# The head of a Mamba block and a mixture of experts: B of the first chunk by TensorE, a split silu

## The chip, the cores and the metric

The kernel runs on one core of one Trainium2 chip. The metric is device time in microseconds (us), the median of several executions. A profile is one more execution, recorded by the hardware profiler.

The engines are TensorE (PE; PEld is its weight load), VectorE (DVE), ScalarE (ACT), GpSimd (POOL) and SyncE (SP), which here only issues transfers (DMAs). Each engine works through its own instructions in the order of the program and waits on semaphores for the others.

## The reference

All arrays are float32; x is 4 x 512 x 256.

```
def mamba(x):                                   # d_inner 512, 16 states, convolution of 4, dt rank 16
    xc, gate = split(x @ in_proj_w.T)
    xt = silu(causal_depthwise_conv(xc) + conv_b)
    ts, B, C = split(xt @ x_proj_w.T, [16, 32])
    dt = softplus(ts @ dt_proj_w.T + dt_proj_b)
    state = state * exp(dt * A) + dt * B * xt   # scanned over the 512 tokens
    y = (state @ C + xt * D) * silu(gate)
    return y @ out_proj_w.T

def moe(x):                                     # 16 experts, the best 4 per token, and a shared one
    ...

x = x + layernorm(mamba(layernorm(x)))
x = x + layernorm(moe(layernorm(x)))
```

## The kernel before

The tokens are cut into 8 tiles of 256 (U), two to a sequence. The 512 channels are four chunks of 128. The scan (L778) works on 128 partitions that hold 32 channels by 4 states; a slot is two such groups of channels by 256 tokens, so that a tile of tokens has 32 slots. For each slot ScalarE computes exp(dt * A) into PSUM (exps, L493), GpSimd multiplies dt * x by B (dbx, L505, one instruction for two slots), VectorE scans (L778) and multiplies by C (hc, L786), and TensorE sums over the states (L800). For this dt and u = dt * x must be spread from 128 channels to 32 channels by 4 states (the tile rep), and B and C from rows to all partitions (bt and ct). Both go through DRAM: stored (L385, L448), then read back with a broadcast (load_rep, L477; load_bc, L470).

Beside the scan of one tile of tokens runs the front of the next ones (norm, in_proj L391, convolution L406, silu L423, x_proj L434, dt_proj L457, softplus L463) and the experts of those before (L1042, L1077 on TensorE; L1049 to L1064 on the others). A planner in the kernel (class Plan) lays down the order of all that from given durations and ranks. It takes the head's state from fixed figures (BUSY) and knows nothing of what the head contains.

The head is written out by hand (function first) and handles tile 0 until its first two slots. In order: layer norm, transposes, taps, in_proj, convolution. Then for both pairs of chunks a sigmoid on ScalarE (two tanh, L414, and one Copy over both chunks that makes 0.5 t + 0.5, L418), then silu on VectorE (L423). A one-element Softplus (L542) loads that table. x_proj (L434) follows, with TensorE's warm-ups (L313, matmuls of the identity) between its parts: four after the second chunk, two after the fourth. Its output becomes ssm on ScalarE (L442): rows of tokens' dt rank, B and C, for the first 128 tokens on the lower 64 partitions and for the others on the upper 64. The store of B and C (L448) and dt_proj (L457) read it. Four more warm-ups into bank f follow, then softplus (L463).

load_bc(0) reads B and C back from DRAM as bt and ct. GpSimd makes u for the first chunk (L553). For this chunk alone dt and u are not spread through DRAM but by TensorE: eight matmuls with a matrix of zeros and ones (rsel, L561) into banks f, h3, y and po, which VectorE copies into rep (L564): f and h3 are dt and u of the first two groups of channels, y and po those of the other two. Then GpSimd multiplies u by B in two halves (inputs_of(0, 2), L505), each for one slot: the first reads what came out of h3, the second what came out of po. Behind them in its queue stand u of the second chunk (L568), the next product (L505), u of the last two chunks (L573), and then the planner's order.

Eight banks of PSUM are in use: three for exps, and f, y, h1, h3 and po, one each; a new tile in a bank waits for the readers of the one before. SBUF tiles come from rings (RINGS): a name has so many buffers, taken in turn.

Of the kernel before, what the change touches and what calls it, by code (L numbers as in the profile page):

```python
# [9 lines left out]
F32 = mybir.dt.float32  # L10
AF = mybir.ActivationFunctionType
ALU = mybir.AluOpType
AX = mybir.AxisListType

P = 128
# [3 lines left out]
R = 16  # L19
# [6 lines left out]
U = 256  # L26
# [4 lines left out]
SS = 4  # L31
CS = P // SS
SG = NS // SS
CG = P // CS
# [14 lines left out]
RINGS = dict(  # L49
    x=3, xr=2, xn=1, xn_t=3, xp=3, sig=2, xt=4, gate=2, ssm=2, dt=1, u=2, mv=6, rstd=6,  # L50
    tail=4, bt=2, ct=2, xg=2, rep=3, delta=3, h=3, dbx=3, hc=11, yg=2, o=1, xn2=1, xn_t2=2, lg=2,
    cw=2, cw_t=1, w13=3, w2=4, cwb=4, th=2, g=3, q=2, res=1, f=1, y=1, h1=1, h3=1, po=1,
)
# [50 lines left out]
    fin=(0.3, 1, 2.2, 1, 0.6, 2.2, 1.5, 0.1),  # L104
)

GROUPS = dict(
    fA=(1, "x stats rstd norm transpose evict"),
    fB=(1, "pad0 in tail conv sigmoid silu xg0"),
# [21 lines left out]
)  # L131
GROUP_OF = {kind: (g, per) for g, (per, kinds) in GROUPS.items() for kind in kinds.split()}


def shift_of(name):
    kind = name[0] + str(name[2]) if name[0] == "xg" else name[0]
    g, per = GROUP_OF[kind]
    n = name[1] // per
    return SHIFTS[g][n] if g in SHIFTS else 0.0, PATIENCE[g][n] if g in PATIENCE else 0.1


class Plan:
# [21 lines left out]

    def add(self, name, eng, dur, rank, fn, deps=(), alloc=(), uses=(), kb=0, done=None):
        shift, patience = shift_of(name)
        rank += shift
        t = dict(
            name=name, eng=eng, dur=dur, rank=rank, fn=fn, deps=[self.names[d] for d in deps],
            alloc=alloc, kb=kb, done=done, at=len(self.tasks), patience=patience,  # L170
        )
        assert name not in self.names, name
        self.names[name] = t
        self.tasks.append(t)
        for key in [key for _, key in alloc] + list(uses):
            self.users.setdefault(key, []).append(t)
        return t
# [70 lines left out]
def mamba_then_moe(ctx: ExitStack, tc: tile.TileContext, a: dict, out: bass.AP):  # L248
    nc = tc.nc
    V, S, G, T = nc.vector, nc.scalar, nc.gpsimd, nc.tensor  # L250
# [5 lines left out]
    work = ctx.enter_context(tc.tile_pool(name="work", bufs=1))  # L256
    dram = ctx.enter_context(tc.tile_pool(name="dram", bufs=N, space=bass.MemoryType.DRAM))
    ps_e = ctx.enter_context(tc.tile_pool(name="ps_e", bufs=RINGS["h"], space=PSUM))
    ps = ctx.enter_context(tc.tile_pool(name="ps", bufs=1, space=PSUM))
# [6 lines left out]
    def load_x(n, what=xs, nm="x"):  # L266
        what[n] = work.tile([P, NU, D], F32, name=nm, bufs=RINGS[nm])
        nc.sync.dma_start(out=what[n], in_=x_in[:, n])
# [21 lines left out]

    rsel = work.tile([P, CG, P], F32, name="w2", bufs=4)
    nc.sync.dma_start(out=rsel, in_=a["rsel"])
    for n in range(1, 3):
        load_x(n)
    w_out = const.tile([P, CI, D], F32, name="w_out")
# [14 lines left out]
    def warm(n, bank):  # L310
        t = ps.tile([P, P], F32, name=bank)
        for _ in range(n):
            T.matmul(t, ident, ident, start=True, stop=True)  # L313
# [6 lines left out]
    hb = const.tile([P, CI], F32, name="hb")  # L320
# [6 lines left out]
    def make_taps():  # L327
        for c in range(CI):
            for k in range(KC):
                V.tensor_scalar_mul(taps[:, c, k, :], ident2, chan[:, c, k : k + 1])  # L330
# [7 lines left out]
    def stats_of(t):  # L338

        st = stat.tile([P, 2, 3], F32, name="st", bufs=RINGS["mv"])  # L340
        V.bn_stats(st.rearrange("p i k -> p (i k)"), t.rearrange("p i d -> p d i"))
        return st
# [21 lines left out]
    live, q = {}, {}  # L364
# [7 lines left out]
    def ring(pool, shape, nm):  # L372
        return pool.tile(shape, F32, name=nm, bufs=RINGS[nm])
# [13 lines left out]
    def in_proj(n, m, bank):  # L387
        t = q["in", n, m] = ps.tile([P, 2, U], F32, name=bank)
        for j in range(2):
            for k in range(CD):  # L390
                T.matmul(  # L391
                    t[:, j, :], w_in[:, k, ts(2 * m + j, P)], q["xn_t", n][:, k, :],
                    start=k == 0, stop=k == CD - 1,
                )
# [16 lines left out]
    def sigmoid(n, m):  # L411
        t = q["sig", n, m]
        for j in range(2):
            S.activation(  # L414
                t[:, j, :], q["conv", n, m][j], AF.Tanh,
                scale=0.5, bias=hb[:, 2 * m + j : 2 * m + j + 1],
            )
        S.activation(t, t, AF.Copy, scale=0.5, bias=0.5)  # L418

    def silu(n, m):  # L420
        t = q["xt", n, m]
        for j in range(2):
            V.scalar_tensor_tensor(  # L423
                t[:, j, :], q["conv", n, m][j], conv_b[2 * m + j], q["sig", n, m][:, j, :],
                ALU.add, ALU.mult,
            )
# [14 lines left out]
    def ssm(n):  # L441
        S.activation(q["ssm", n], q["x", n], AF.Identity, bias=one_row)  # L442
# [40 lines left out]
    def place(k):  # L483

        return k // SLOTS, k // CSL % CI, k // CP % SG, k % CP
# [9 lines left out]
        for j in range(1, NJ):  # L495
            S.copy(h[:, j, 0:1], zero)  # L496

    def inputs_of(k, parts=1):

        n, c, g, _ = place(k)  # L500
        t = dbxs[k // CP] = ring(work, [P, CG, U], "dbx")
        bt = live[n]["bt"][:, g, :].unsqueeze(1).to_broadcast([P, CG, U])
        for i in range(parts):
            m = ts(i, CG // parts)
            G.tensor_tensor(t[:, m], reps[n * CI + c][:, m, 1, :], bt[:, m], ALU.mult)  # L505
        if n % UB:
            G.tensor_tensor(t[:, :, 0], t[:, :, 0], deltas[n * CI + c][:, g, :], ALU.add)

    def first():
        st = stats_of(xs[0])  # L510
        rstd = stat.tile([P, NU], F32, name="rstd")
        G.tensor_scalar(rstd, st[:, :, 2], 1.0 / D, EPS, ALU.mult, ALU.add)
        G.tensor_tensor(rstd, rstd, mhalf, ALU.pow)
        xn = ring(work, [P, NU, D], "xn")
        for i in range(NU):
            V.tensor_scalar(
                xn[:, i, :], xs[0][:, i, :], st[:, i, 1:2], rstd[:, i : i + 1],
                ALU.subtract, ALU.mult,
            )
        xn_t = q["xn_t", 0] = ring(work, [P, CD, U], "xn_t")  # L520
        for k, nm in enumerate(("f", "h1")):
            t = ps.tile([P, U], F32, name=nm)
            for i in range(NU):
                T.transpose(t[:, ts(i, P)], xn[:, i, ts(k, P)], ident)
            (V.tensor_copy if k else S.copy)(xn_t[:, k, :], t)
        make_taps()
        for m in range(2):
            in_proj(0, m, ("h3", "y")[m])
        for m in range(2):
            xp = q["pad", 0, m] = ring(work, [P, 2, KC - 1 + U], "xp")  # L530
            G.memset(xp[:, :, 0 : KC - 1], 0.0)
            copy = V.tensor_copy if m else S.copy
            copy(xp[:, :, KC - 1 :], q["in", 0, m])
            t = tails[1, m] = ring(stat, [P, 2, KC - 1], "tail")
            copy(t, q["in", 0, m][:, :, U - KC + 1 :])
        for m in range(2):
            conv(0, m, (("po", "f"), ("h1", "h3"))[m])
        for m in range(2):
            sigmoid(0, m)
        for m in range(2):  # L540
            silu(0, m)
        S.activation(spare, zero, AF.Softplus)  # L542
        x_proj(0, "y", lambda c: warm(5 - c, "f"))
        ssm(0)
        store_bc(0)
        rp = reps[0] = ring(work, [P, CG, 2, U], "rep")
        us = [ring(work, [P, 2, U], "u") for m in range(2)]
        dt_proj(0, ("po", "h1"))
        warm(4, "f")
        softplus(0)  # L550
        dt = [q["sp", 0][:, ts(m, 2), :] for m in range(2)]
        load_bc(0)
        G.tensor_tensor(us[0][:, 0, :], dt[0][:, 0, :], q["xt", 0, 0][:, 0, :], ALU.mult)  # L553

        banks = iter("f h3 y po".split())
        spread = {}
        for h in range(2):
            for w, src in enumerate((dt[0][:, 0, :], us[0][:, 0, :])):
                t = spread[h, w] = ps.tile([P, 2, U], F32, name=next(banks))
                for j in range(2):  # L560
                    T.matmul(t[:, j, :], rsel[:, 2 * h + j, :], src, start=True, stop=True)  # L561
        for h in range(2):
            for w in range(2):
                V.tensor_copy(rp[:, ts(h, 2), w, :], spread[h, w])  # L564
        for i in range(2):
            exps(i)
        inputs_of(0, 2)
        G.tensor_tensor(us[0][:, 1, :], dt[0][:, 1, :], q["xt", 0, 0][:, 1, :], ALU.mult)  # L568
        for w, t in enumerate((dt, us)):
            nc.sync.dma_start(out=live[0]["rep"][1, :, w], in_=t[0][:, 1, :])  # L570
        load_rep(1)
        inputs_of(CP)
        G.tensor_tensor(us[1], dt[1], q["xt", 0, 1], ALU.mult)  # L573
        live[0]["dt and u"] = dt[1], us[1]
# [245 lines left out]
    for k in range(N * SLOTS):  # L820
        n, c, g, p = place(k)
# [4 lines left out]
        if k % CSL == 0:  # L826
            if i > 1:
                m = c // 2
# [448 lines left out]
```

## Time and profile before

| what | us |
|---|---|
| median of 3 runs | 696.59 (696.58 to 697.05) |
| profiled execution | 697.16 |
| span of its instructions | 695.0 |
| TensorE busy | 675.1 (97%) |
| GpSimd busy | 602.3 (87%) |
| VectorE busy | 579.0 (83%) |
| ScalarE busy | 495.6 (71%) |

A row of the timeline has the start from the span's start, the duration (of several merged instructions from the first start to the last end), the engine, the line of the kernel, the operation, what it writes and reads, the shape and the count. In brackets stands how long the engine sat idle before it, and what ended that. fp32 matmuls show as two passes each. The profile leaves numbers out of names, so the banks h1 and h3 and those of exps are all h. Busy slices are tenths of 40 equal parts of the span.

### The profile page before, as it was taken

To read this page: it belongs to the slowest core of one execution; us is meant where nothing else is said; L and a number is where in the kernel's file an instruction comes from. 1 tells how busy PE (TensorE), PEld (TensorE's weight loads), DVE (VectorE), ACT (ScalarE), POOL (GpSimd) and SP (SyncE) were. 2 spreads that over 40 slices of the span, in tenths; PEclk is the share of its full clock that TensorE was granted. 3 is DMA by queue.
4 is the path that set the end of the run, shared out by engine and by line. 5 is a ranking of instruction groups with operands and counts; after the bars stand their busy time and mean duration, and the time that the engine had idled before them with its cause. 6 is when DMAs were issued, how large, how long until landed. Compare 5 with 4: busy or idle time off the path is not lost.

```text
span 695.0 us, 13317 instructions
## 1 busy us (share of the span) xinstructions
PE 675.1 (97%) x4462; PEld 537.3 (77%) x4462; DVE 579.0 (83%) x819; ACT 495.6 (71%) x1308; POOL 602.3 (87%) x607
## 2 busy tenths in 40 slices
PE   8999898999999999999999999999999999999997
PEld 7767676777778677877777788787777787878886
DVE  3699999999999899899999999889999979952112
ACT  2799979898768778877888867877777757734320
POOL 1498669999999999999999999999999999985553
PEclk9999999999999999999999999999999999999999
DMA  5398675596866696787678867786787864664561
GB/s 167 108 318 299 223 231 194 160 296 186 289 240 209 199 309 234 229 298 248 200 237 289 272 175 232 232 269 223 246 265 227 288 222 138 205 198 143 181 207 46
DMA packets 84696, 155.15 MB, mean 223 GB/s; under 512 B 9842, under 2 KB 33266, under 8 KB 84628
## 3 DMA queue, kind: packets, MB, share of 16 engines
q1 hardware_dynamic: 83796, 152.99, 67.6%
q10 hardware_dynamic: 832, 1.31, 0.5%
q8 instruction: 35, 0.57, 0.3%
q14 instruction: 33, 0.27, 0.1%
HBM read 135.27 MB, written 19.01 MB: 222 GB/s over the span
## 4 chain that ended last, share of the span: by engine, by line
PE 50%; ACT 6%; DVE 5%; POOL 5%; issue 2%; DMA 2%; POOLq 0%; SPq 0%; DVEq 0%; ACTq 0%
PE h L1042 26%; PE po L1077 12%; PE y L800 4%; ACT h L493 3%; PE f L895 3%; DVE h L778 2%; POOL dbx L505 2%; DVE hc L786 2%; PE f L1077 1%; PE f L391 1%; DMA w<-in_w 1%; PE f L406 1%; DMA cwb<-cwd 1%; PE f L934 1%; POOL g L1064 1%
## 5 line engine op out<-in xcount | busy, mean ns | idle before, releaser
L778 DVE TENSOR_TENSOR_SCAN h<-h,dbx 128x512 f32<-128x512 f32 x256 | 308.4, 1220 | 12.2 <-ACT h L496 6.4
L505 POOL TENSOR_TENSOR dbx<-rep,bt 128x1024 f32<-128x1024 f32 (+1 forms) x129 | 302.3, 2347 | 16.5 <-DVE h L778 13.0
L1042 PE MATMUL h<-xn_t,w 128*128 128x256 f32 x1280 | 296.0, 382 | 0.2
L493 ACT ACTIVATE h<-rep,a_rep 128x256 f32<-128x256 f32 x512 | 244.5, 478 | 54.5 <-DVE hc L786 42.6
L1042 PEld LDWEIGHTS h<-xn_t,w 128*128 128x128 f32 x1280 | 239.5, 190 | 43.4 <-issue 4.4
L786 DVE TENSOR_TENSOR hc<-h,ct 128x512 f32<-128x512 f32 x256 | 171.0, 681 | 3.7 <-ACT carry L790 0.9
L1077 PE MATMUL po<-w,g 128*128 128x256 f32 x600 | 144.2, 382 | 1.0 <-POOL g L1064 0.9
L1077 PEld LDWEIGHTS po<-w,g 128*128 128x128 f32 x600 | 111.5, 190 | 22.7 <-POOL g L1064 4.0
L1064 POOL TENSOR_TENSOR g<-g,q 128x512 f32<-128x512 f32 x80 | 101.8, 1272 | 5.2 <-DVE q L1061 2.5
L1057 POOL TENSOR_TENSOR g<-g,cwb 128x512 f32<-128x512 f32 x64 | 81.5, 1273 | 19.4 <-ACT g L1054 15.4
L1061 DVE SCALAR_TENSOR_TENSOR q<-th,h 128x512 f32<-128x512 f32 x80 | 54.4, 680 | 49.4 <-PE h L1042 40.5
L1049 ACT ACTIVATE th<-h 128x512 f32<-128x512 f32 x80 | 47.5, 593 | 39.0 <-PE h L1042 38.7
L800 PE MATMUL y<-hc,sel 128*32 128x256 f32 x1024 | 67.5, 385 | 0.0
L800 PEld LDWEIGHTS y<-hc,sel 128*32 128x32 f32 x1024 | 27.5, 109 | 29.0 <-issue 14.8
L496 ACT COPY h<-zero 128x1 f32<-128x1 f32 x256 | 41.7, 163 | 8.2
L391 PE MATMUL f<-xn_t,w_in 128*128 128x256 f32 x176 | 42.6, 385 | 2.4 <-DVE gate L740 1.3
L1054 ACT COPY g<-h 128x512 f32<-128x512 f32 x64 | 37.1, 579 | 9.2 <-PE f L1077 8.7
L391 PEld LDWEIGHTS f<-xn_t,w_in 128*128 128x128 f32 x176 | 32.6, 190 | 10.3 <-DVE gate L740 1.5
L790 ACT COPY carry<-h 128x2 f32<-128x2 f32 x128 | 19.7, 160 | 19.3 <-DVE hc L786 13.7
L406 PE MATMUL h<-xp,taps 64*64 64x256 f32 x288 | 29.5, 381 | 0.8 <-DVE xt L423 0.8
L895 PE MATMUL f<-w_out,yg 128*128 128x256 f32 x112 | 26.5, 383 | 1.0 <-DVE xt L423 1.0
L406 PE MATMUL f<-xp,taps 64*64 64x256 f32 x208 | 25.4, 382 | 1.7 <-DVE xt L423 0.9
(169 smaller groups left out, 623.4 us busy)
## 6 DMA issues: line engine op xcount, KB each, us to landing
w<-in_w SPq DMA_DIRECT2D x80, 512.0 KB, 5.0
rep<-rep SPq DMA_DIRECT2D x124, 256.0 KB, 4.7
w<-in_w SPq DMA_DIRECT2D x80, 256.0 KB, 4.4
cwb<-cwd SPq DMA_DIRECT2D x64, 256.0 KB, 5.3
xg<-xg SPq DMA_DIRECT2D x32, 256.0 KB, 4.4
bt<-bc SPq DMA_DIRECT2D x8, 512.0 KB, 6.0
ct<-bc SPq DMA_DIRECT2D x8, 512.0 KB, 6.8
xg<-xt SPq DMA_DIRECT2D x16, 256.0 KB, 4.5
```

The lines of the kernel that those rows point to most:

```text
L391: T.matmul(t[:, j, :], w_in[:, k, ts(2 * m + j, P)], q["xn_t", n][:, k, :], start=k == 0, stop=k == CD - 1,)
L406: T.matmul(t[j][half[r ^ j], :], taps[half[r], 2 * m + j, k, :], q["pad", n, m][half[r], j, k : k + U], start=k == 0, stop=k == KC - 1,)
L493: S.activation(h[:, j, :], dt[:, m, 0, :], AF.Exp, scale=a_rep[:, c, g, m : m + 1])
L505: G.tensor_tensor(t[:, m], reps[n * CI + c][:, m, 1, :], bt[:, m], ALU.mult)
L778: V.tensor_tensor_scan(flat, flat, dbx[:, ts(p, NJ), :].rearrange("p j t -> p (j t)"), 0.0, ALU.mult, ALU.add)
L786: V.tensor_tensor(hc, expo[k], ct, ALU.mult)
L800: T.matmul(ys[n, c][m * CS : (m + 1) * CS, :], sel, hcs[k][:, j, :], start=g == 0, stop=g == SG - 1,)
L1042: T.matmul(t[:, j, :], weights[i][:, j, ts(CD * w + k, P)], x[:, k, :], start=k == 0, stop=k == CD - 1,)
L1057: G.tensor_tensor(gs[i], gs[i], cws[i], ALU.mult)
L1061: V.scalar_tensor_tensor(t, hid[i, "th"], 1.0, hid[i, 1], ALU.add, ALU.mult)
L1064: G.tensor_tensor(gs[i], gs[i], hid[i, "q"], ALU.mult)
L1077: T.matmul(acc[n][t] if n == N - 1 else acc[n][:, t, :], gs[i][:, j, ts(t, P)], weights2[i][:, j, :], start=m == 0 and j == 0 and (t == 0 ...
```

## The change

There are two edits in the head. First, the sigmoid and the silu of the first pair of chunks now come before those of the second pair. Of the second pair, VectorE scales the first chunk's tanh (a TENSOR_SCALAR) and ScalarE the second's (a Copy over 256 columns instead of 512).

Second, B of the first group of states is brought to the scan's partitions by TensorE: two matmuls with a matrix of zeros and ones (bsel, 128 x 256, one half for each half of the tokens) read ssm and write bank f, and VectorE copies that to SBUF (first_b). The two halves of GpSimd's first product read first_b in the place of bt. The four warm-ups into f that stood there become two into y. bsel is loaded behind rsel in SP's queue, into a buffer of the ring q, and first_b takes one of the ring th. bt and ct are still stored and loaded, for the products that follow. An empty table of corrections to the planner's ranks (NUDGES) changes nothing. The planner's order is that of before on every engine.

```diff
@@ the loads @@
     nc.sync.dma_start(out=rsel, in_=a["rsel"])
+
+    bsel = work.tile([P, 2, P], F32, name="q", bufs=RINGS["q"])
+    nc.sync.dma_start(out=bsel, in_=a["bsel"])
     for n in range(1, 3):
         load_x(n)
@@ inputs_of @@
-    def inputs_of(k, parts=1):
+    def inputs_of(k, parts=1, b=None):
...
-        bt = live[n]["bt"][:, g, :].unsqueeze(1).to_broadcast([P, CG, U])
+        bt = (live[n]["bt"][:, g, :] if b is None else b).unsqueeze(1).to_broadcast([P, CG, U])
@@ first @@
-        for m in range(2):
-            sigmoid(0, m)
-        for m in range(2):
-            silu(0, m)
+        sigmoid(0, 0)
+        silu(0, 0)
+
+        sig = q["sig", 0, 1]
+        for j in range(2):
+            S.activation(sig[:, j, :], q["conv", 0, 1][j], AF.Tanh, scale=0.5, bias=hb[:, 2 + j : 3 + j])
+        V.tensor_scalar(sig[:, 0, :], sig[:, 0, :], 0.5, 0.5, ALU.mult, ALU.add)
+        S.activation(sig[:, 1, :], sig[:, 1, :], AF.Copy, scale=0.5, bias=0.5)
+        silu(0, 1)
         S.activation(spare, zero, AF.Softplus)
         x_proj(0, "y", lambda c: warm(5 - c, "f"))
@@ first @@
         dt_proj(0, ("po", "h1"))
-        warm(4, "f")
+        b0 = ps.tile([P, U], F32, name="f")
+        for h in range(2):
+            T.matmul(b0[:, ts(h, U // 2)], bsel[:, h, :], q["ssm", 0], start=True, stop=True)
+        first_b = ring(work, [P, U], "th")
+        V.tensor_copy(first_b, b0)
+        warm(2, "y")
         softplus(0)
@@ first @@
-        inputs_of(0, 2)
+        inputs_of(0, 2, first_b)
@@ kernel @@
+    row = np.arange(P)[:, None, None] - (R + 1) - P // 2 * np.arange(2)[:, None]
+    arrays["bsel"] = (row == SG * (p % SS)).astype(np.float32)
```

## The prediction

> **What bounds the kernel now.** I read the granted clock first (span 695.0 us, mean clock 0.999, so nothing here is a throttle), then the busy slices, then the timeline of the first 45 us engine by engine, then the chain that ended last.
>
> ```profile
> span 695.0 us, 13317 instructions
> ...
> DVE  3699999999999899899999999889999979952112
> ...
> POOL 1498669999999999999999999999999999985553
> ```
>
> A slice is 17.4 us. The change touches slices 1 and 2 (up to 29.8 us); from slice 3 on VectorE and GpSimd are nearly full, and the chain that ended last, which the profile can follow back to 201.9 us, passes between ScalarE, VectorE, GpSimd and TensorE and lies on TensorE nearly without a break from 391 us. So no engine's sum is touched; the question is how much earlier the full stretch starts and whether that shift reaches the end.
>
> The timeline of GpSimd and VectorE around the start of the scan:
>
> ```profile
> 26.69 2.50 POOL L505 TENSOR_TENSOR dbx<-rep,bt 128x512 f32<-128x512 f32 x2 [2.98 <-DMA bt<-bc]
> 29.14 0.73 POOL L568 TENSOR_TENSOR u<-dt,xt 128x256 f32<-128x256 f32 x1
> 29.82 2.36 POOL L505 TENSOR_TENSOR dbx<-rep,bt 128x1024 f32<-128x1024 f32 x1
> 32.14 1.27 POOL L573 TENSOR_TENSOR u<-dt,xt 128x512 f32<-128x512 f32 x1
> ```
>
> ```profile
> 24.98 0.69 DVE L564 COPY rep<-h 128x512 f32<-128x512 f32 x1 [0.17 <-PE h L561]
> 25.85 0.69 DVE L564 COPY rep<-y 128x512 f32<-128x512 f32 x1 [0.17 <-PE y L561]
> 26.71 0.69 DVE L564 COPY rep<-po 128x512 f32<-128x512 f32 x1 [0.17 <-PE po L561]
> 27.32 0.69 DVE L341 BATCH_NORM_STATS2 st<-x 128x6 f32<-128x512 f32 x1
> 27.99 2.46 DVE L778 TENSOR_TENSOR_SCAN h<-h,dbx 128x512 f32<-128x512 f32 x2
> ...
> 37.62 2.35 DVE L778 TENSOR_TENSOR_SCAN h<-h,dbx 128x512 f32<-128x512 f32 x2 [0.66 <-POOL dbx L505]
> ```
>
> GpSimd waits 2.98 for the transfer of bt, and then runs without a wait until 54.8. VectorE waits for it at 37.62 (0.66) and at 41.47 (0.33), then does not idle until 64.3. So until 41.5 us GpSimd's start sets the pace, and what counts is when its second half-multiply (27.91 to 29.18, the second of the x2) ends.
>
> **The silu split.** The old order on ScalarE is two tanh (to 17.99), one Copy over 512 columns (18.02 to 18.65), then VectorE's two silu steps (18.68 to 19.56). The new one: VectorE is free of the first pair at 17.83 and scales one half in 0.41 (the row of TENSOR_SCALAR 128x256, L516), to about 18.16; ScalarE scales the other half in about 0.40 (between the 512-column Copy's 0.63 and the 128-column L442's 0.37), to about 18.43; the silu steps of 0.48 end near 18.65 and 19.06, 0.50 earlier. Does x_proj (L434) start earlier?
>
> ```profile
> 18.25 1.16 PE L313 MATMUL f<-ident 128*128 128x128 f32 x8
> 19.34 0.71 PE L434 MATMUL y<-xt,w_x 128*64 128x128 f32 x8
> ...
> 53.42 1.09 PE L434 MATMUL f<-xt,w_x 128*64 128x128 f32 x16
> ```
>
> Hardly. The four warm-ups that x_proj issues after its first two chunks fill TensorE; their last matmul starts at 19.14, and every change of the tile's width costs 0.20 from start to start (18.05 to 18.25, 19.78 to 19.98, 21.51 to 21.71, in narrow windows), which gives 19.34, the start seen. The data of the third chunk had been there since 19.17. Only the fourth waits: 19.61 is the silu's end at 19.56 plus 0.05. The uninterrupted run at 53.42 moves a pair each 0.11 us, so eight of its matmuls take 1.09 - 4 x 0.11 = 0.65, against 0.71 here. The split is worth **0.06**, not 0.50; the cover is the warm-ups, and without them it would be worth up to 0.50. ssm's ACTIVATE starts 0.05 after x_proj's end (20.05 to 20.10) and moves with it; the table load before it, now from 18.45, ends at 19.73 and is off the path. dt_proj follows x_proj's warm-ups by the same 0.20 and moves by 0.06 too.
>
> **The copy of B by TensorE.** Removed: four warm-ups (eight passes, 21.71 to 22.60 by starts). Added: two fp32 matmuls of bsel with ssm (four passes of the warm-ups' shape, 0.11 each) and two warm-ups (four passes): eight passes for eight. b0's last pass ends at 21.65 + 0.21 + 2 x 0.11 + 0.28 = 22.36; VectorE, idle until 24.12, copies 128x256 out of PSUM. By the same shape (L525: 0.42) bank f is free at 22.82, 0.10 before the spread's first matmul (22.98 - 0.06), which waits for softplus. By the larger shape (128x512: 0.69) it would be free at 23.09, and the spread would lose 0.2. I take 0.42 and **0**.
>
> POOL's first multiply no longer waits for bt, whose stores left at 20.49 and which landed at 26.6. It now waits for the copies of rep: the first half for that of h, which ends at 25.61, the second for that of po, which ends at 27.34 (27.40 - 0.06). From a VectorE end to a GpSimd start the trace shows 0.09 (63.31 to 63.40) to 0.14 (60.40 to 60.54). First half: 25.72 to 26.99. Second: 27.45 + 1.27 = 28.72, against 29.18: **0.46 earlier**, between 0.43 and 0.48. The first half gains 0.97, but waiting for po takes half of that back. The floor is set by the copies; with the copies 0.2 late the gain is 0.26.
>
> VectorE gains less at first. The first scan stands behind bn_stats and starts 0.11 earlier; the second, which waited for 29.18, about 0.2. At 37.62, though, VectorE has 0.66 of idle: bn_stats ends there at 36.96 less 0.2 to 0.3, GpSimd's product at 37.59 - 0.46 = 37.13, so the scan moves by the whole 0.46, and so does the one at 41.47. ScalarE's norm at 35.00 waits for GpSimd's rstd and moves with it; the load of the second rep stands behind the store of u (29.90, after POOL L568) and moves too.
>
> Hidden additions: bsel's issue joins SP's queue after rsel (5.60) and pushes two x loads, w_out and w_r by one issue (0.43). SP's last of these ended at 8.92 and SP is then idle to 20.49; x is first read at 27.32, and an x load lands in at most 8.1. bsel itself, issued near 6.0, is read at 21.65. GpSimd's second product (29.3) now carries the wait for bt, 2.7 after it lands. Behind those waits stand all of GpSimd's products, so each cover would cost one for one if it went. The order on all five queues after the head is the same.
>
> One rule speaks against this edit, since the first half-multiply now runs beside copies on VectorE. In before the first half starts at 26.69, the copy of po at 26.71, and that copy takes 0.69 like the three others: no blocking. The Trainium skill's page SBUF — State Buffer (Who interferes with whom) says that a copy or tensor_scalar on VectorE can take ports that it shares with GpSimd and that the later of the two then waits; by that the copy of y would wait for the half-multiply. The skill's page VectorE: DVE Perf Modes (Why PSUM operands drop a tier) exempts operands in PSUM, which these copies read, and the trace agrees (0.69 beside GpSimd and alone).
>
> **Sum.** 0.46 earlier. The profiled execution took 697.16 (span 695.0 and 2.2 around it): 696.70. The median of the runs is 696.59, 0.57 below it: **696.13**, 0.07% faster. About 0.2% (1.4 us) is what a measurement of this kernel can tell from no change, so this counts as the same.
>
> **Rivals.**
> - *The shift is absorbed* (0.15): somewhere later the chain rests on work that did not move. Against it: every engine and SP depend on GpSimd's chain by 41.5 us. Time 696.6.
> - *The split pays* (0.05): x_proj follows the silu after all and everything moves by 0.50 rather than 0.06, 0.90 in all: 695.7. Against it: the 0.20 after each change of tile width.
> - *The copy of y waits for GpSimd* (0.03), the slower end. It decides as soon as the half-multiply starts before the copy of y does (25.72 against 25.79). y then starts at 26.99, po ends at 28.3, the second half runs 28.4 to 29.7: 0.5 later than before: 697.1. The copy of po at 26.71 speaks against it.
> - *Transfers on the chain meet others.* The chain holds a load of weights (318.8, 5.66 to landing; loads near it 5.8 to 6.5, median of all 5.0) and one of cwb (326.1, 4.99; median 5.3). Worse (0.12): 0.84 + 0.31 - 0.46 = +0.7, 697.3. Better (0.08): 0.66 + 0.46 = 1.1 less, 695.5. For it: even unchanged, the runs spread by 0.47.
>
> **How the numbers follow.** Forecast 0.57 at 696.13. The range 695.4 to 697.2 leaves out about half of the transfer cases. A change of over 1.4 us needs two of these together: faster 0.07, slower 0.07, same 0.86.
>
> **What would show it.** Right: x_proj's second part still at 19.34 and ending near 20.00; the spread at 22.92; half-multiplies at 25.7 and 27.45; the waits of VectorE for GpSimd near 37.2 and 41.0; the same offset of about 0.45 at 200 and 600 us. Wrong: a spread later than 22.98 (the copy of b0 is longer), copies of rep over 0.69, or an offset that dies or grows between 41 us and the end.

## The result and the profile after

| | us |
|---|---|
| changed kernel, median of 20 runs | 695.67 (694.91 to 696.48) |
| kernel before beside it, median of 20 runs | 696.65 (696.20 to 698.01) |
| ratio | 0.9985, 95% interval 0.9978 to 0.9992 |
| profiled execution, before and after | 697.16 and 695.37 |
| span of its instructions, before and after | 695.0 and 693.6 |

The changed kernel takes 1.0 us less (by the interval 0.5 to 1.5), where 0.46 was forecast (696.13). The class, within 0.2%, and the range hold; the size was about half. A second set of runs of the same two kernels gave 696.09 against 696.99 (0.9987, 0.9979 to 0.9996).

The head first. GpSimd's products (lines of the changed kernel: dbx is L512, the spread's copies are L581, x_proj is L441, the scan is L795):

```profile
24.83 1.27 POOL L512 TENSOR_TENSOR dbx<-rep,th 128x512 f32<-128x512 f32 x1 [2.06 <-DVE rep L581]
26.55 1.28 POOL L512 TENSOR_TENSOR dbx<-rep,th 128x512 f32<-128x512 f32 x1 [0.46 <-DVE rep L581]
27.79 0.73 POOL L585 TENSOR_TENSOR u<-dt,xt 128x256 f32<-128x256 f32 x1
```

In the old profile one merged pair waited 2.98 for the transfer of bt. Now the halves stand apart, and both wait for VectorE's copies, as the forecast had it. VectorE beside them:

```profile
24.92 0.69 DVE L581 COPY rep<-y 128x512 f32<-128x512 f32 x1 [0.17 <-PE y L578]
25.78 0.69 DVE L581 COPY rep<-po 128x512 f32<-128x512 f32 x1 [0.17 <-PE po L578]
```

```profile
36.28 2.35 DVE L795 TENSOR_TENSOR_SCAN h<-h,dbx 128x512 f32<-128x512 f32 x2 [0.53 <-POOL dbx L512]
...
40.13 1.23 DVE L795 TENSOR_TENSOR_SCAN h<-h,dbx 128x512 f32<-128x512 f32 x1 [0.32 <-POOL dbx L512]
```

The copy of y starts 0.09 after GpSimd's first half and takes its usual 0.69. The two waits of VectorE for GpSimd are still there (0.66 and 0.33 before), so GpSimd's lead passes on to the scan whole.

Absolute times can't be compared between these profiles: everything, the first transposes too, starts 0.88 earlier. TensorE's first rows, of before and then of after, show why:

```profile
1.34 7.48 PE L313 MATMUL f<-ident 128*128 128x128 f32 x40 [1.34 <-POOL ident masks.py:199]
8.88 0.44 PE L524 MATMUL f<-ident,xn 128*128 128x128 f32 x2
```

```profile
1.34 6.60 PE L320 MATMUL f<-ident 128*128 128x128 f32 x40 [1.34 <-POOL ident masks.py:199]
8.00 0.44 PE L531 MATMUL f<-ident,xn 128*128 128x128 f32 x2
```

These are 20 warm-ups, 40 passes, which nothing in the change touches. A pass takes 0.21 us until some moment and 0.11 after it; that moment was 7.05 us in the one execution and 5.32 in the other. The granted clock's row shows full speed throughout, but the clock records kept with the traces begin only at 7.12 and 5.29 us, and the row counts the time ahead of the first record as full speed. So I count from the first matmul of the convolution (13.43 us before, 12.55 after). Counted so, the starts of the scan's slots against those of before, and what lies around the span (the execution's time less the span, from its result):

| kernel | slot 1 | slot 9 | slot 65 | slot 73 | slot 201 | slot 209 | slot 256 | convolution to end | around the span |
|---|---|---|---|---|---|---|---|---|---|
| before | 0 | 0 | 0 | 0 | 0 | 0 | 0 | 681.55 | 2.18 |
| after | -0.10 | -0.46 | -0.43 | -0.69 | -0.76 | -0.62 | -0.61 | 681.09 | 1.73 |
| after again (c1) | -0.10 | -0.43 | -0.41 | -0.67 | -0.62 | -0.47 | -0.36 | 681.36 | 1.73 |
| before again (c0) | 0.05 | 0.07 | 0.11 | 0.11 | 0.19 | 0.20 | 0.42 | 681.99 | 2.20 |
| B alone (e1) | -0.04 | -0.40 | -0.36 | -0.61 | -0.43 | -0.38 | -0.25 | 681.41 | 1.78 |
| silu alone (e2) | -0.08 | -0.06 | -0.02 | -0.02 | 0.05 | 0.15 | 0.29 | 681.87 | 1.91 |

At slot 9 the forecast's 0.46 is there to the hundredth. The last column holds the surprise: 0.45 us of the gain lie outside of the span, where nothing was forecast to change.

### The profile page after: what moved, and what is told of

The parts are those of the page before. It is cut to its first block, busy times and chain, and to the rows that moved or that the text cites. A ratio compares the mean times of both kernels' runs of the same rounds, so it can differ in the third digit from the quotient of the medians.

```text
span 693.6 us, 13321 instructions
## 1 busy us (share of the span) xinstructions
PE 674.0 (97%) x4462; PEld 536.5 (77%) x4462; DVE 579.3 (84%) x821; ACT 495.5 (71%) x1308; POOL 602.5 (87%) x607
## 4 chain that ended last, share of the span: by engine, by line
PE 48%; DVE 10%; ACT 7%; POOL 3%; issue 2%; DMA 1%; POOLq 0%; DVEq 0%; ACTq 0%
PE h L1059 25%; PE po L1094 12%; DVE h L795 5%; PE y L817 4%; ACT h L500 3%; DVE hc L803 3%; PE f L912 2%; POOL dbx L512 1%; PE f L1094 1%; PE f L398 1%; DVE q L1078 1%; DMA rep<-rep 1%; PE f L413 1%; ACT h L503 1%; PE f L951 0%
## 5 line engine op out<-in xcount | busy, mean ns | idle before, releaser
L795 DVE TENSOR_TENSOR_SCAN h<-h,dbx 128x512 f32<-128x512 f32 x256 | 308.5, 1221 | 12.0 <-ACT h L503 6.4
L512 POOL TENSOR_TENSOR dbx<-rep,bt 128x1024 f32<-128x1024 f32 x127 | 299.6, 2362 | 13.3 <-DVE h L795 12.8
```

What stands on the lines that cost most here:

```text
L795: V.tensor_tensor_scan(flat, flat, dbx[:, ts(p, NJ), :].rearrange("p j t -> p (j t)"), 0.0, ALU.mult, ALU.add)
```

## The experiments

Each kernel was timed beside the kernel before on the same chip. The first four shared one set (before: 697.09, 33 runs), c0 to e6 a second (696.99, 30 runs), e7 to e10 a third (696.96, 33 runs). The theory at the outset was the forecast's: the head's 0.46 and nothing else. Its rivals: an effect of the edits that it left out, and chance at the start.

**e1 and e2: each edit alone.** e1 is the changed kernel with the old order of sigmoid and silu; e2 is the kernel before with the new order.

```diff
# e1, against the changed kernel
-        sigmoid(0, 0)
-        silu(0, 0)
...
-        silu(0, 1)
+        for m in range(2):
+            sigmoid(0, m)
+        for m in range(2):
+            silu(0, m)
```

> Only the second edit (B by TensorE); the old order of sigmoid and silu. Theory 1 (the recorded one): GpSimd's second half-multiply is held by the copy of po, and ends 0.40 earlier against the start of the convolution than in before; the time falls by 0.40. In the profile: x_proj's eight last matmuls take 0.71 from first start to last end, as in before. Theory 2 (the measured 1.0 is what the change is worth, through something the prediction left out): the time falls by about 0.9 to 1.0 with this edit alone. Theory 3 (the start of the head differs from execution to execution, by the moment at which TensorE's warm-ups go to full speed, whatever the kernel): the first transposes start anywhere from 8.0 to 8.9 us, and the span follows that start one for one.

> Only the first edit (order of sigmoid and silu, the split Copy). Theory 1: x_proj's second part still starts 0.20 after the last warm-up and takes 0.65 instead of 0.71; the time falls by 0.06. Rival (the split pays by itself): x_proj ends 0.5 earlier and the time falls by 0.3 to 0.5. Theory 2 would need 0 to -0.1 here if the rest is in the other edit, or up to -0.6 here.

e1: 696.01, ratio 0.9988 (0.9979 to 0.9997). e2: 696.56, 0.9994 (0.9986 to 1.0003). In the traces both are as theory 1 has them: 0.40 and 0.06 at slot 9. In the times both gained more (1.08 and 0.53, so 0.68 and 0.47 beyond that), with intervals too wide to decide. The table's last column has more than half of the rest: 0.40 and 0.27 around the span.

**e3 and e4: does a larger lead at the head pay?** e3 spreads dt and u of the second half in the other order, so that the operand that GpSimd waits for is copied third and not last. e4 leaves out the four warm-ups after x_proj's second chunk and keeps the two after the fourth; no result depends on warm-ups.

```diff
# e3
-        for h in range(2):
-            for w, src in enumerate((dt[0][:, 0, :], us[0][:, 0, :])):
+        for h, w in ((0, 0), (0, 1), (1, 1), (1, 0)):
+            src = (dt, us)[w][0][:, 0, :]
# e4
-        x_proj(0, "y", lambda c: warm(5 - c, "f"))
+        x_proj(0, "y", lambda c: warm(2 if c == 3 else 0, "f"))
```

> The changed kernel with one thing more: the spread of the second two groups of channels is done for u before dt (both its matmuls and its copy), so that GpSimd's second half-multiply waits for the third copy and not the fourth. Theory 1 (GpSimd's chain sets the pace to 41 us and its shift reaches the end): the two half-multiplies run back to back, the second ends 0.50 earlier than in the changed kernel, VectorE's wait of 0.53 before the scan of slot 4 shrinks to about 0, and the time falls by 0.5 against the changed kernel, about 1.0 to 1.5 against before. Rival (VectorE's or ScalarE's own queue is the bound there; the exps of slot 1 come 0.86 later): no gain against the changed kernel, or up to 0.3 slower.

> The changed kernel without the four warm-ups that x_proj issues after its second chunk (their matmuls compute nothing that is used). Theory 1 (those warm-ups cover the silu split): x_proj's second part starts as soon as the third silu is done and ends about 0.5 earlier; ssm then waits for the load of the Softplus table and moves by 0.2, dt_proj no longer waits for the change of the tile's width and moves by 0.29, and the time falls by 0.29 against the changed kernel. Rival (x_proj is held by something else, or TensorE loses speed without the warm-ups): no change, or slower matmuls in dt_proj and the spread (passes of 0.21 where they take 0.11), 1 us or more.

e3: 695.93 (0.9983, 0.9974 to 0.9991). e4: 695.72 (0.9981, 0.9972 to 0.9990). In e3 GpSimd's two halves run back to back and the second ends 0.50 earlier than in the changed kernel, as expected; at slot 9 0.30 of that is left, and e4 leads there by 0.23. TensorE of e4 shows that the forecast's cover was the right one:

```profile
18.18 0.83 PE L441 MATMUL y<-xt,w_x 128*64 128x128 f32 x8 [0.35 <-DVE xt L430]
```

Without the warm-ups x_proj waits for the silu, and starts 0.66 earlier after the convolution (5.25 against 5.91). At the end of both profiles, however, the extra lead was gone: from the convolution 681.10 and 681.09, against 681.09 for the changed kernel. I took that for absorption by a TensorE-bound tail. The next runs refuted it.

**c0 and c1: both kernels once more, unchanged.**

> The kernel before once more, unchanged, as a null. What is to be told apart: the medians of the first runs fell by about 0.5 to 0.65 us more than the head of their traces accounts for, in the kernel with the silu split alone as well. Theory 1 (the kernels truly differ, partly in where TensorE's step to the full pace falls or in later slots): ratio 1.000 (within 0.0005) against the other runs of the kernel before. Rival (the kernel before reads too high where it is the baseline): this copy reads 0.3 to 0.6 us less than the baseline, ratio 0.9992 or below. In its trace, if the moment of the full pace is only chance, the first transposes may start anywhere from 8.0 to 8.9 us and the span follows them one for one; if it belongs to the kernel, they start at 8.8 to 8.9 again. The 0.28 us wait of GpSimd for a transfer near slot 66 of the scan comes again if it belongs to the kernel.

> The changed kernel once more, unchanged. Theory 1: 1.0 us below the baseline (0.9985, within 0.0005), of which 0.46 us is the head; from the convolution to the end 681.1 us within 0.2. Theory 3 (chance of the start): the start of the convolution differs from 12.55 us by up to 0.9 us and the span with it, one for one.

c0: 697.31, 1.0003 (0.9994 to 1.0012), so the baseline reads true. c1: 696.09, 0.9987 (0.9979 to 0.9996). In both profiles the step to the faster pass fell at 6.63 us and the transposes started at 8.65, so the start is chance and not the change. With that equal, the spans differ by 0.63 (695.19 and 694.56) and the times by 1.10 (697.39 and 696.29). The first profile of the changed kernel had been 0.27 luckier after the convolution than this one, which is why e3 and e4 had seemed to bring nothing.

**e5 and e6: the start, and the three leads together.** e5 is the changed kernel with 16 initial warm-ups; e6 adds the edits of e3 and e4 (its expectation miscounts the warm-ups inside x_proj, where two stay of six, and what it calls the spread of B is that of dt and u).

```diff
-    warm(20, "f")
+    warm(16, "f")
```

> The changed kernel with 16 in place of 20 warm-up products ahead of the first transposes; nothing of the computation is left out. Theory 3 (the initial warm-ups hold the first transposes when TensorE's step to the full pace falls late): 8 passes at 0.21 us would end 1.7 us earlier, so that the transposes wait for the normalised input alone (8.04 to 8.44 us in the six traces so far) in every execution: the slow half of the runs gains up to 0.6 us, the fast half nothing, median 0.2 to 0.3 us below the changed kernel, and the spread of the times narrows. Rival: with fewer warm-ups the step to the full pace comes later, falls among the transposes, and the kernel takes 0.5 to 2 us more.

> The changed kernel with three more edits: 16 initial warm-ups, two in place of fourteen warm-ups inside the first x_proj, and the spread of B in the order that brings the second half's operands first; nothing of the computation is left out. The head alone gives 0.5 us more at the eighth slot of the scan. Theory (the middle and the tail are bound by other things, and a lead beyond about 0.5 us at the head is given back after slot 200): the same time as the kernel with 16 initial warm-ups within 0.2 us. Rival (a lead at the head reaches the end): 0.5 us below it.

e5: 695.70 (0.9976, 0.9967 to 0.9985), all runs within 695.13 and 695.86, where c1's reach from 695.39 to 697.00. e6: 695.17 (0.9973, 0.9963 to 0.9983). e6's profile catches the late case: the step fell at 6.59, as in c1, and yet the transposes wait only for their data.

```profile
1.35 6.30 PE L320 MATMUL f<-ident 128*128 128x128 f32 x32 [1.35 <-POOL ident masks.py:199]
7.97 0.56 PE L531 MATMUL f<-ident,xn 128*128 128x128 f32 x2 [0.32 <-DVE xn L523]
```

They start at 7.97, against 8.65 in c1. And e6 is 0.53 below e5 (681.33 and 680.81 from the convolution in the profiles): the rival was right, a lead at the head reaches the end.

**e7 to e9: the change without the chance of the start.** e7 is the kernel before with 16 initial warm-ups; e8 and e9 repeat e5 and e6 beside it.

> The kernel before with 16 in place of 20 initial warm-up products; nothing of the computation is left out. If the late step to the full pace holds the first transposes in the kernel before as in the changed one, it gains 0.3 to 0.6 us on the kernel before and its times spread by 0.8 us instead of 1.6. Its difference to the changed kernel with 16 warm-ups (run beside it) is then the change without the chance of the start: 0.46 us by the forecast's head alone, 0.7 us with the transfer near slot 66 that no longer holds GpSimd; a difference near 1.0 would mean that a part of it lies outside of what the traces show.

> The changed kernel with 16 initial warm-ups again, beside the kernel before with 16: 0.46 us below it (head alone) or 0.7 (head and slot 66); 1.2 to 1.4 us below the baseline, as at its first run.

> The combined kernel again. A lead at the head reaches the end: 0.5 us below the changed kernel with 16 warm-ups. It is given back: no difference beyond 0.2 us.

e7: 696.69 (0.9995, 0.9987 to 1.0004), runs within 0.76. It is 0.27 below the kernel before, where 0.3 to 0.6 was expected, and the interval includes no gain. e8: 695.78 (0.9982, 0.9973 to 0.9991). e9: 695.29 (0.9978, 0.9969 to 0.9987). The change is worth 0.91 here, near the expectation's third case. The time around the span is 2.19 in e7 (2.14 to 2.24 in eleven runs) and 1.70 in e8 (1.68 to 1.74): that is 0.49, and the median spans differ by 0.4 (694.5 and 694.1). e9 is 0.49 below e8, as a lead that reaches the end should be (0.27 by the two profiles, from the convolution to the end).

e8's slowest run, 696.33, is the profiled one, and it shows that fewer warm-ups don't end all chance of the start:

```profile
8.91 0.56 PE L531 MATMUL f<-ident,xn 128*128 128x128 f32 x2 [1.64 <-DVE xn L523]
```

Here the step wasn't late (5.76 us), but VectorE's wait for its first load ended at 6.33, against 5.33 in e5, and the transposes start at 8.91 against 7.92.

**e10: fewer warm-ups still.** e6 with `warm(12, "f")`.

> The combined kernel with 12 instead of 16 initial warm-ups, nothing left out: 24 passes of at most 0.21 us end by 5.5 us, 2.5 us before the transposes can start. If the warm-ups only have to have ended by then: the same time as with 16. If TensorE needs them up to the full pace: where that comes late, the step is put off by a whole period (3.4 us), the transposes run at half pace, and the kernel takes 1 to 3 us more in some runs or all.

696.24 (0.9988, 0.9978 to 0.9998): five runs at 694.98 to 695.49, as good as e9, and six at 696.24 to 697.91, with a mean granted clock down to 0.993. The second case came true in half of the runs. That these met the step a period late is argued from their times; the profiled execution was one of the good five. In it the clock records begin at 6.97 us, after the last warm-up has started (6.41) and before the transposes (8.22).

## Where the time went, and why the forecast was half of it

**The head: right, step by step.** TensorE and VectorE of the changed kernel:

```profile
18.46 0.66 PE L441 MATMUL y<-xt,w_x 128*64 128x128 f32 x8
...
22.05 1.10 PE L578 MATMUL f<-dt,w 128*128 128x256 f32 x4
```

```profile
21.53 0.42 DVE L565 COPY th<-f 128x256 f32<-128x256 f32 x1 [3.40 <-PE f L563]
```

x_proj's second part starts 5.91 after the convolution before and after, and takes 0.66 (forecast 0.65), so the silu split is worth 0.05 to 0.06; the rival in which it pays is refuted (its 695.7 is near the measured time by coincidence), and e4 shows that the warm-ups hid it. The copy of b0 took 0.42 and was covered: the spread starts 9.50 after the convolution, against 9.55. GpSimd's second half ends 0.47 earlier (15.75 to 15.28). The scan's first two slots gain 0.10 and 0.20, as forecast, and the fifth 0.46. The blocked copy did not come.

**The shift reaches the end: right, but not by itself.** Two places change the lead on its way. Between slots 65 and 73 it grows by 0.25. In all four profiles of kernels with the old B, GpSimd idles 0.28 to 0.32 ahead of its 38th product (the two halves counted), the one for slots 73 and 74, and no releaser explains it (c0 here; the instruction named had ended 0.30 before). The expectations call this a transfer near slot 66, but no row names a transfer as what GpSimd waits for.

```profile
175.08 0.74 POOL L818 TENSOR_TENSOR yg<-xg 128x256 f32<-128x256 f32 x1
176.12 2.37 POOL L505 TENSOR_TENSOR dbx<-rep,bt 128x1024 f32<-128x1024 f32 x1 [0.30 <-POOL yg L818]
```

In none of the ten with the new B does it (c1):

```profile
174.57 0.74 POOL L835 TENSOR_TENSOR yg<-xg 128x256 f32<-128x256 f32 x1
175.31 2.36 POOL L512 TENSOR_TENSOR dbx<-rep,bt 128x1024 f32<-128x1024 f32 x1
```

The delay is passed on through xr, which GpSimd makes further down its queue. VectorE waits for it ahead of the scan of slot 71 in the kernel before, and not in the changed one:

```profile
183.62 0.71 DVE L341 BATCH_NORM_STATS2 st<-xr 128x6 f32<-128x512 f32 x1 [0.32 <-POOL xr L911]
```

```profile
182.01 0.71 DVE L348 BATCH_NORM_STATS2 st<-xr 128x6 f32<-128x512 f32 x1
```

Then, just ahead of slot 204, about 0.14 is given back. VectorE there, before and after:

```profile
497.05 0.09 DVE L964 MATCH_VALUE_LOAD rest<-top,lg 128x8 f32 x1
497.13 0.17 DVE L964 MATCH_REPLACE8 rest<-top,lg 128x20 f32<-128x20 f32 x1
```

```profile
495.42 0.09 DVE L981 MATCH_VALUE_LOAD rest<-top,lg 128x8 f32 x1
495.81 0.17 DVE L981 MATCH_REPLACE8 rest<-top,lg 128x20 f32<-128x20 f32 x1 [0.29 <-issue]
```

"issue" means that the engine waited for nothing that the profile shows. Which instruction it strikes follows VectorE's count, not the work. The change adds three instructions to VectorE's program, B alone one, the silu alone two. In e2 and e1 the stall sits on two other instructions of the same group:

```profile
497.11 0.09 DVE L969 MATCH_VALUE_LOAD rest<-top,lg 128x8 f32 x1 [0.17 <-issue]
```

```profile
496.40 0.17 DVE L976 MATCH_REPLACE8 rest<-top,lg 128x20 f32<-128x20 f32 x1 [0.21 <-issue]
```

In all eleven profiles of kernels that add instructions to VectorE it is the 832nd that VectorE executes, counted in the trace. In the kernel before, that one is the scan behind the group, which pauses 0.09. In thirteen of the fourteen profiles an 8 KB instruction fetch starts 0.67 to 0.71 us after it starts (1.47 in e6).

Two rivals of the forecast can be settled here too. The shift is not absorbed (e6 and e9). And the transfers near 320 us changed nothing that shows: between slots 73 and 201 (188 and 490 us in the kernel before) the lead changes by 0.03 to 0.09 in the three pairs of profiles, before and after, c0 and c1, e7 and e8.

**The step that failed: "697.16 (span 695.0 and 2.2 around it)".** The sum carried the 2.2 over unchanged. It is a constant of a kernel, within 0.1 us of its median over its runs (the spans are rounded to 0.1), and it moved, by the medians: 2.19 before, 1.80 with B alone, 1.90 with the silu alone, 1.71 with both. The trace of DMA traffic in the window from 692 to 698 us (a slice is 0.15 us; of before, then of after) shows one more transfer, an instruction fetch and the only one on queue q14, after the last instruction:

```profile
DMA  0001994189400000000000000000002000000000
...
q14 instruction: 1, 0.01, 0.5%
```

```profile
DMA  5000000000000002000000000000000000000000
...
q14 instruction: 1, 0.01, 0.5%
```

It is the lone digit after the burst of the outputs: in the slice from 696.5 in the one (whose span ends at 694.98) and from 694.25 in the other (693.64). By the trace's records the fetch starts 1.62 after the span's end before, 1.37 in e2, 1.16 in e1 and 0.63 after. In the changed kernel fetches start 0.69, 0.67 and 0.65 us after the starts of VectorE's 832nd, 960th and 1088th instructions, so here one comes every 128. The 1088th is its last, and there the fetch after the span comes soonest. In the kernel before, VectorE's count ends at 1085.

So three more instructions on VectorE go with a fetch that starts 1.0 us sooner after the span and with an execution that ends 0.47 sooner after it. That the one brings the other is argued, and two things don't fit a simple rule. B alone adds one instruction and the silu alone two, yet B alone has the earlier fetch and the larger gain. And in e10, which has VectorE's 1088 as well, the fetch starts 0.90 after the span's end, while the time around the span is 1.72 as in the others.

The Trainium skill's page Runtime: NRT & Kernel Launch (Instruction fetch mechanics) says that each engine fetches its own program block by block while it runs, mostly hidden. The even distance agrees with that; the page's block is 256 instructions in 16 KiB, where the trace shows 128 and 8 KB. "Mostly" is here 0.17 to 0.29 us at the 832nd instruction in the eleven profiles, and 0.09 in the kernel before.

**The balance**, from e7 and e8, where the warm-ups don't hold the transposes: 0.49 around the span, and 0.4 in it by the medians. That is 0.9 of 0.91 measured. The part in the span is, by the table, 0.46 at the head, 0.25 more by slot 73, 0.14 less at slot 204, and a rest towards the end that differs from profile to profile. From the convolution to the end the three pairs of profiles give 0.46, 0.63 and 0.65 (681.66 and 681.02 for e7 and e8), and the two profiles of the kernel before differ by 0.44 there.

So the forecast's 0.46 was right for the head by its mechanism, and near the span's gain partly by luck. It had named "an offset that dies or grows between 41 us and the end" as a sign of being wrong, and in the three pairs the offset grew to between 0.76 and 0.95 by slot 201; much of the growth was then given back. The other half of the measured gain lies around the span, which the sum had left as it was.

**What stays open.** That the time around the span hangs on VectorE's count and not on GpSimd's, which goes from 846 to 845 with the new B, rests on the silu edit alone: e2 leaves GpSimd's count as it was and yet gains 0.29. No kernel only changed a count, so it is argued from fourteen profiles and not shown by one edit. GpSimd's idle 0.3 ahead of its 38th product strikes its 197th instruction in the kernels with 846 and is absent with 845. The next 8 KB fetch starts 1.9 to 2.1 us after that instruction, not 0.7, so the traces don't tie it to a fetch, and its cause stays open.

**The best version.** The combined kernel (e6, e9) beats both: 695.17 and 695.29, ratios 0.9973 and 0.9978 to the kernel before, and 0.8 to 0.9 below the changed kernel of c1. Of that, 0.5 is the two edits at the head and 0.3 to 0.4 the four warm-ups that no longer hold the transposes.

## What to carry to other kernels

Compare profiles from a landmark behind the chance of the start, and take two profiles of a kernel before a difference of 0.3 us is read from them. Put the time around the span into the sum as a term of its own: here edits that add one to three instructions went with 0.3 to 0.5 us less of it, as much as the edits themselves were worth or more, and moved VectorE's short pause as well. Where a gain is hidden by filler work such as warm-ups, try the edit together with less filler.

## What was not expected of the hardware

TensorE's step from 0.21 to 0.11 us a pass came between 4.28 and 7.05 us in the profiles in which it was seen, and moved the whole kernel by up to 0.9 us. The Trainium skill's page TensorE: Matmul & The Clock Gate (Part 1: The HAM clock gate) says that the window that decides this runs freely and is not set back when a kernel starts. The traces agree: the warm-ups start at 1.34 or 1.35 us in all of them, and the step does not follow that. 20 warm-ups were too many here where the step was late; 16 held the transposes in none of the five profiles that have them; with 12, six runs of eleven took 696.24 or more. The row of the granted clock doesn't show this step, since it has no record from before it.
